# Row minima of two strips by ScalarE copies and GpSimd halvings, every block transpose on VectorE, row buffers as scratch for the late spans: one change to a four-layer network kernel

## The chip, the cores and the metric

The kernel runs on one core of one Trainium2 chip. The metric is the device time of one execution in microseconds; the figure for the kernel before is the median of three runs. A core has TensorE (PE: matrix products, results into PSUM), VectorE (DVE), ScalarE (ACT), GpSimd (POOL, which here works only on SBUF tiles) and SyncE (SP, which issues the transfers). Each engine takes its own instructions strictly in the order written and waits on semaphores for the others.

## The reference

A sequence of 2048 tokens of 128 numbers passes through four layers. Each layer adds an attention of a layer-normalised x to x, and then adds a feed-forward of a layer-normalised x.

- L0: full softmax attention, 16 heads of 64; then a mixture of 8 experts with a capacity limit.
- L1: causal attention, 16 heads of 64; then a gated mix of each token with the token before it (`r * (relu(k)^2 @ W_v)`).
- L2: an "attention" whose query and key terms are such that the kernel needs only one 128x128 product per token (the folded matrix `w2`); then a feed-forward of width 512 with ternary weights and ReLU.
- L3: full attention with a region mask and a bias per head and query from five small feature networks; then a feed-forward of width 512 with binarised weights and an exact GELU.

For full attention with queries q, keys k and values v of one head:

```
scores[i, j] = q_i . k_j / 8        (+ mask, + bias)
p[i, :]      = exp(scores[i, :] - max_j scores[i, j])
out[i]       = sum_j p[i, j] v_j / sum_j p[i, j]
```

Everything is float32 except small mask tiles.

## The kernel before

**Attention.** Heads go two at a time: 8 pairs in each of the layers L0, L1 and L3. In a pair, class `Pair` makes kT, qT and v from the normalised, transposed x (`projected`, L450 and `valued`, L471). The queries of a pair are cut into 8 groups of 256, and a group into 8 strips of 32 queries. Class `Group` holds the work of one group. So a full layer has 64 groups, the two full layers (L0 and L3) 128.

The kernel keeps scores negated (qT is multiplied by -scale), so that the row maximum of the softmax is a row minimum here. The keys are spread out: partition block c (of four, 32 partitions each) holds the 32 queries of the strip against every fourth block of 32 keys, 512 of the 2048 keys. For one strip and one head the scores are thus a PSUM bank of 128 partitions by 512.

The steps of a group, with the lines that the profile names:

1. `score` / `make` (L556, PE): two strips times two heads fill four PSUM banks. The ring `BANKS` has just four.
2. `scan` (L566, DVE): one instruction per strip and head copies the bank into the row buffer `e` in SBUF and takes the minimum of each row at the same time, into `low`. 16 scans in a group.
3. `spread_lowest`: POOL sets the four partition blocks' minima side by side (L613), DVE reduces them (L616), in L3 POOL subtracts and adds the bias (L620, L621), and ACT (in L1 POOL) hands the result out to the partition blocks (L627). Once for strips 0 to 3 (j = 0) and once for strips 4 to 7 (j = 1).
4. `exps` (L639, ACT): exponentials in place, with row sums, 16 in a group.
5. `turn` (L666, DVE): the exponentials are transposed in 32x32 blocks in place. There is one call per half (j) and head (h), 128x2048 each. In the full layers the last of the four calls (j = h = 1, `apart`) does only 384 of the 512 columns of each strip, 128x1536; the other 128 columns go through four PE transposes (L674) and an ACT copy back from PSUM (L677). A PE transpose gives another order of the keys in the partitions, so those columns need a copy `va` of the values with rows in that order: `regroup` (L485, POOL), 16 small copies per pair.
6. `weigh` (L698, PE): values times turned exponentials, accumulated in the bank `o`, in four steps of eight matmuls.
7. `sum_up` (L719 and POOL's power L739), the copy oT (L771, ACT), the output projection (L756, PE), the division (L766, ACT) and the addition to x (L784, POOL).

**Between L1 and L3** the tokens go in spans of 4, 4, 4, 2 and 2 tiles of 128. Each span runs `first_norm`, then `rest`: the gated mix of L1, the product of L2, the ternary feed-forward, and three more calls of `normalise`; at the end stands the x that L3's keys and queries are made of. L3's softmax needs all keys, so its first score waits for the last span. Scratch tiles come from rings with few buffers: `MIXED` 3 (one span takes all three), `PAIRED` 2, `MID` 4, and the PSUM ring `MISC` 3. `features` makes L3's bias from the same x, in four chunks. At the end of the program `final` runs L3's feed-forward over the same spans.

`normalise` takes statistics on DVE (L301 to L303), then three POOL instructions (add epsilon L306, power -1/2 L307, multiply by minus the mean L308), then scales on ACT (L311) and on DVE or POOL (L316), transposes on PE (L322) and copies to xT on ACT (L337).

**The order of the work** is not written out by hand. Every step is an object with an engine, an assumed duration, what it needs and which ring buffers it takes. A planner (`run`) plays a list schedule forward and ranks the steps backward from their latest starts, three times over, and the best of these gives the order in which each engine's instructions are written. `planner(tick, place)` gives the first rank. So a change of a step's engine or assumed cost can move instructions everywhere.

Of the kernel before, what the change touches and what calls it, by code (L numbers as in the profile page):

```python
# [13 lines left out]
ALU = mybir.AluOpType  # L14
AX = mybir.AxisListType

P = 128
# [41 lines left out]
def network(ctx: ExitStack, tc: tile.TileContext, a: dict, out: bass.AP):  # L59
# [26 lines left out]
    class Held:  # L86


        def __init__(self, ring, called=None):
            self.ring, self.called, self.users = ring, called, []  # L90

    class Step:
        def __init__(self, key, engine, us, do, after=(), takes=(), uses=(), then=None, table=None):
            self.key, self.engine, self.us, self.do, self.takes = key + (len(steps),), engine, us, do, takes
            self.table = table
            self.after, self.order, self.then, self.end = list(after), [], then, None
            for h in takes:
                h.by = self
                h.users.append(self)
                h.ring.takers.append(self)  # L100
            for h in uses:
                self.after.append(h.by)
                h.users.append(self)
            steps.append(self)
# [15 lines left out]
    def run():  # L120
# [101 lines left out]
        for _ in range(3):  # L222
            rank = backward()
            if not forward(rank, False):
                break
            found.append((max(s.end for s in steps), len(found), rank))
# [13 lines left out]

    MISC = Ring(ps_t, "t", [P, 512], 3, ordered=False)
# [8 lines left out]
    APART = Ring(work, "va", [P, 4, DH], 2)  # L250
# [43 lines left out]
    def normalise(add, t0, n, after, before=(), row=None, hurry=False):  # L294


        mv, xn, pt = Held(MEANS), Held(NORMED), Held(MISC, "pt")

        def stats(i):
            st = small.tile([P, 6], F32, tag="st", name="st")  # L300
            nc.vector.bn_stats(out=st, in_=x[:, t0 + i, :])  # L301
            nc.vector.bn_aggr(out=mv.t[:, i, 0:2], in_=st)
            nc.vector.tensor_scalar(mv.t[:, i, 3:4], mv.t[:, i, 0:1], -1.0, None, ALU.mult)  # L303
# [20 lines left out]
        made = [add(DVE, 0.6, lambda: stats(0), after, takes=[mv])]  # L324
        made += [add(DVE, 0.6, lambda i=i: stats(i), after, uses=[mv]) for i in range(1, n)]
        power = add(POOL, 1.65, powers, made, uses=[mv])
        scales = [add(ACT, 0.45, lambda: scaled(0), [power], takes=[xn], uses=[mv])]
        for i in range(1, n):
            if i < n // 2:
                scales.append(add(ACT, 0.4, lambda i=i: scaled(i), [power], uses=[mv, xn]))  # L330
            elif hurry:
                scales.append(add(DVE, 0.3, lambda i=i: scaled_on(nc.vector, i), [power], uses=[mv, xn]))
            else:
                scales.append(add(POOL, 0.8, lambda i=i: scaled_on(nc.gpsimd, i), [power], uses=[mv, xn]))
# [20 lines left out]
    class Attention:  # L355
# [31 lines left out]
        def course(self, p):  # L387
# [15 lines left out]
            if p == HP - 1:  # L403
                groups = [(g, 4 * g, 4 * g + {0: 12, 1: 10}.get(g, 8)) for g in range(NS)]
                return groups, 0, (-5, 3, 11, 19), steady, (9, 13, 18, 24)
# [11 lines left out]
        def left(self, t0, n):  # L417

            groups = self.course(HP - 1)[0]
            g, _, weigh = groups[(t0 + n - 1) // 2]  # L420
            return self.begin + 32 * (HP - 1) + weigh + (g // 2 + 1 if self.causal else 4) + 1
# [4 lines left out]
    class Pair:  # L426
# [39 lines left out]
        def valued(self, add, c):  # L466
# [13 lines left out]
            if c == 3 and not self.layer.causal:  # L480
                self.va = Held(APART)

                def regroup(i):
                    for q in range(4):
                        nc.gpsimd.tensor_copy(self.va.t[bass.ts(i, Q), q, :], v.t[bass.ts(q, Q), i, DH:P])  # L485

                self.va_made = [
                    add(
                        POOL, 1.0, lambda i=i: regroup(i), self.v_made[3:],
                        takes=[] if i else [self.va], uses=[v, self.va] if i else [v],  # L490
                    )
                    for i in range(4)
                ]

    class Group:
# [37 lines left out]
        def score(self, add, add_scan, k):  # L533
# [47 lines left out]
            for i in range(2):  # L581
                for h in range(2):
# [5 lines left out]
                    (uses if k % 2 or i or h else takes).append(self.lows[j])  # L588
                    found.append(
# [4 lines left out]
            return found  # L594

# [57 lines left out]
        def apart(self, j, h):  # L653

            return j == h == 1 and not self.layer.causal

        def turn(self, add, j, h, made):


            n = self.width(4 * j) - (P if self.apart(j, h) else 0)  # L660

            def rows():
                return self.e(h)[:, bass.ts(j, 4), :]

            def do():
                nc.vector.transpose(rows()[:, :, 0:n], rows()[:, :, 0:n])  # L666

            turned = [add(DVE, 0.05 + 0.00426 * n, do, made, uses=self.rows)]
            if self.apart(j, h):
                pt = Held(MISC)  # L670

                def turn_apart():
                    for i in range(4):
                        nc.tensor.transpose(pt.t[:, bass.ts(i, P)], rows()[:, i, n : n + P], ident)  # L674

                def copy():
                    nc.scalar.copy(rows()[:, :, n : n + P], pt.t.rearrange("p (i n) -> p i n", i=4))  # L677

                add(PE, 0.55, turn_apart, made, takes=[pt], uses=self.rows)
                turned.append(add(ACT, 0.47, copy, uses=[pt] + self.rows))  # L680
            return turned

        def weigh(self, add, c, turned):
# [7 lines left out]
            def do():  # L691
                for t in ts:
                    for h in range(2):
                        parts = [(first(t), NS, self.pair.v[c].t[:, t % 4, bass.ds(DH * h, DH)])]
                        if c == 3 and self.apart(1, h):
                            parts = [(0, 4, parts[0][2]), (4, NS, self.pair.va.t[:, t % 4, :])]
# [11 lines left out]
            if c == 3 and self.apart(1, 1):  # L708
                uses, made = uses + [self.pair.va], made + self.pair.va_made
# [323 lines left out]
    def feed_forward(add, t0, n, after, full, w1T, b1, func, w2T):  # L1033

        hT, made, po = [Held(MID, "hT") for f in range(NC)], [], Held(MISC, "po")
        for f in range(0, NC, 2):
            ph = [Held(MISC, "ph") for k in range(2)]
# [121 lines left out]
    def rest(add, t0, n, done, hurry, made):  # L1159
        m = P * n  # L1160
        xr, xk, ka, r = Held(MIXED, "xr"), Held(MIXED, "xk"), Held(MIXED, "ka"), Held(PAIRED, "r")
        pk, pr, pv, po = (Held(MISC, n) for n in ("pk", "pr", "pv", "po"))
# [24 lines left out]
        for to, part, mu in ((xk, rests[1], mu_k), (xr, rests[0], mu_r)):  # L1187
# [44 lines left out]
        done, rows = normalise(add, t0, n, [full], read, row=ob2, hurry=hurry)  # L1232
# [5 lines left out]
        done, rows = normalise(add, t0, n, [full] + rows, [attended], row=b2_2, hurry=hurry)  # L1238
# [3 lines left out]
            lambda: ternary_w.t[:, 0:FF], b1_2, AF.Relu, lambda: ternary_w.t[:, FF : 2 * FF],  # L1242
# [3 lines left out]
        done, rows = normalise(add, t0, n, [full] + rows, firsts, row=ob3, hurry=hurry)  # L1246
# [132 lines left out]
    mix_spans = [(0, 4), (4, 4), (8, 4), (12, 2), (14, 2)]  # L1379
# [7 lines left out]
    for t0, n in mix_spans:  # L1387
# [3 lines left out]
    for t0, n in mix_spans:  # L1391
        rest(planner(L1.left(t0, n)), t0, n, done[t0], n < 4, made)
    feature_reads = []
    for c in range(4):
        seen = len(steps)
        features(planner((L1.left(8, 4) - 1, L1.left(12, 2) - 1, L1.left(14, 2) + 1, L1.left(14, 2) + 2)[c]), c)
# [95 lines left out]
```

## Time and profile before

| what | value |
|---|---|
| time, median of 3 runs | 3460.41 us (3458.63 to 3462.35) |
| the profiled execution: time, and span from first to last instruction | 3458.86 us, 3457.2 us |
| busy: PE, DVE, ACT, POOL | 3371.3, 3216.3, 2801.9, 950.9 us |
| L0, four pairs from 392.94 to 983.91 us | 147.74 us per pair |
| L3, two pairs from 2350.89 to 2649.92 us | 149.5 us per pair |
| end of L1's last `weigh` to L3's first score | 2120.09 to 2204.46 us |

The span is the time between the first and the last instruction of one profiled execution; the rest of that execution's time lies around it. A record of a matmul has a modelled end, and one float32 product shows as two records, so counts of PE instructions in the profile are twice those of the program. Durations of neighbouring instructions overlap a little in the records; the distance from start to start is what an instruction really takes from its engine. A group's idle time is the idle time of its engine just before it, with what ended it.

### The profile page before, as it was taken

The page shows a single profiled execution, that of the slowest core. Times are in us where ns is not written, and L with a number is a line of the kernel's source. Part 1 is how long each engine was busy: PE and PEld are TensorE (multiplying, and loading weights), DVE is VectorE, ACT ScalarE, POOL GpSimd, SP SyncE. Part 2 cuts the span into 40 slices and gives each one's busy share as a digit, 9 for nine tenths or more (in the row PEclk, how much of TensorE's full clock was granted, in tenths as well). Part 3 has the DMA queues.
Part 4 walks back from the last instruction along what each step waited for, and adds up shares of the span by engine and source line. Part 5 has one row for each costly group of instructions (what it writes and reads, how often), then busy time and mean ns, then how long its engine had stood idle before and what let it go on. Part 6 is the DMA issues. An engine that isn't in the chain of part 4 may idle for free.

```text
span 3457.2 us, 115453 instructions
## 1 busy us (share of the span) xinstructions
PE 3371.3 (98%) x46922; PEld 1808.7 (52%) x46922; DVE 3216.3 (93%) x8019; ACT 2801.9 (81%) x8707; POOL 950.9 (28%) x2821
## 2 busy tenths in 40 slices
PE   8999999999999998999999997899999999999999
PEld 3544444545445454555655654455555555555555
DVE  7999999999999989899999884699999999999996
ACT  6788888888888777788888985678888888888886
POOL 2121221222222343233233353222222222222233
PEclk9999999999999999999999998899999999999999
DMA  1000000000000000000000000000000000000000
GB/s 48 2 5 2 5 5 2 5 2 5 2 5 5 2 5 8 6 6 6 6 6 3 9 2 4 4 5 5 2 5 2 5 5 2 5 2 2 2 5 11
DMA packets 22961, 18.98 MB, mean 5 GB/s; under 512 B 3557, under 2 KB 21613, under 8 KB 22427
## 3 DMA queue, kind: packets, MB, share of 16 engines
q1 hardware_dynamic: 22362, 11.55, 1.2%
q8 instruction: 367, 6.01, 0.7%
q14 instruction: 168, 1.37, 0.1%
q0 software_dynamic: 64, 0.06, 0.0%
HBM read 10.60 MB, written 1.05 MB: 3 GB/s over the span
## 4 chain that ended last, share of the span: by engine, by line
PE 83%; DVE 12%; ACT 3%; issue 2%; POOL 0%; DMA 0%; SPq 0%; DVEq 0%; POOLq 0%; ACTq 0%
PE s L556 33%; PE o L698 32%; DVE e L566 6%; PE pp L450 5%; DVE e L666 4%; PE y L756 3%; PE pv L471 3%; PE t L674 2%; ACT e L639 1%; PE ps L719 1%; PE pe L999 1%; PE ph L1041 1%; PE po L1066 1%; PE pt L322 0%; DVE st L301 0%
## 5 line engine op out<-in xcount | busy, mean ns | idle before, releaser
L639 ACT ACTIVATE e<-e,shift 128x512 f32<-128x512 f32 (+15 forms) x3072 | 1972.7, 648 | 23.7 <-POOL shift L627 16.4
L566 DVE TENSOR_SCALAR_CACHE_REDUCE e<-s 128x512 f32<-128x512 f32 (+15 forms) x3072 | 1660.5, 590 | 77.9 <-PE s L556 75.1
L556 PE MATMUL s<-kT,qT 64*32 64x512 f32 (+8 forms) x24576 | 1448.9, 533 | 17.7 <-DVE e L566 16.4
L666 DVE STREAM_TRANSPOSE e<-e 128x2048 f32<-128x2048 f32 (+10 forms) x768 | 1436.8, 1873 | 18.8 <-ACT e L639 18.0
L698 PE MATMUL o<-e,v 128*64 128x256 f32 (+1 forms) x10496 | 1275.4, 374 | 6.6 <-DVE e L666 6.4
L698 PEld LDWEIGHTS o<-e,v 128*64 128x64 f32 x10496 | 738.4, 137 | 565.5 <-issue 309.3
L556 PEld LDWEIGHTS s<-kT,qT 64*32 64x32 f32 x24576 | 413.7, 105 | 527.0 <-DVE e L566 218.0
L639 ACT ACTIVATION_READ_ACCUMULATOR e<-e,shift 128x1 f32 x3072 | 592.3, 193 | 0.0
L613 POOL COPY low<-low 32x8 f32<-32x8 f32 x1152 | 208.1, 181 | 1336.3 <-DVE e L566 1238.9
L784 POOL TENSOR_TENSOR x<-x,part 128x256 f32<-128x256 f32 x384 | 280.5, 730 | 359.2 <-ACT part L766 338.2
L627 ACT COPY shift<-shift 32x8 f32<-32x8 f32 x768 | 150.0, 195 | 178.9 <-POOL shift L621 98.5
L766 ACT ACTIVATE part<-y,r 128x128 f32<-128x128 f32 x768 | 220.6, 360 | 42.7 <-PE y L756 38.4
L566 DVE DVE_READ_ACCUMULATOR e<-s 128x1 f32 x3072 | 235.0, 76 | 0.0
L450 PE MATMUL pp<-xT,w 128*128 128x512 f32 x384 | 212.7, 646 | 2.5 <-ACT xT L337 1.9
L698 PE MATMUL o<-e,va 128*64 128x128 f32 x1024 | 196.4, 274 | 0.0
L739 POOL TENSOR_TENSOR r<-r,inverse 128x4 f32<-128x4 f32 x128 | 130.2, 1017 | 171.6 <-ACT r L742 169.7
L771 ACT COPY oT<-o 128x256 f32<-128x256 f32 x192 | 71.0, 370 | 125.1 <-PE o L698 124.6
L556 PE MATMUL s<-beyond,eye 64*32 64x32 bf16 x2560 | 158.2, 176 | 0.0
L756 PE MATMUL y<-w,oT 64*128 64x128 f32 x1536 | 137.9, 297 | 1.0 <-ACT oT L771 0.7
L756 PEld LDWEIGHTS y<-w,oT 64*128 64x128 f32 x1536 | 100.9, 186 | 57.5 <-issue 46.5
L698 PEld LDWEIGHTS o<-e,va 128*64 128x64 f32 x1024 | 126.8, 138 | 0.0
L556 PEld LDWEIGHTS <-regions 64*32 64x32 bf16 x1024 | 65.3, 93 | 112.2 <-issue 78.5
(190 smaller groups left out, 2055.0 us busy)
## 6 DMA issues: line engine op xcount, KB each, us to landing
w<-in_L_wq SPq DMA_DIRECT2D x24, 64.0 KB
w<-in_L_wk SPq DMA_DIRECT2D x24, 64.0 KB, 2.1
w<-in_L_wv SPq DMA_DIRECT2D x24, 64.0 KB
w<-in_L_wo SPq DMA_DIRECT2D x24, 64.0 KB, 2.1
x<-in_x SPq DMA_DIRECT2D x4, 256.0 KB, 4.8
out_x<-x SPq DMA_DIRECT2D x3, 256.0 KB
wo<-in_L_wo SPq DMA_DIRECT2D x1, 512.0 KB
moe_w<-in_moe_w SPq DMA_DIRECT2D x1, 512.0 KB
```

The source lines that it names most:

```text
L450: nc.tensor.matmul(pp.t, lhsT=self.w.t[:, which, :], rhs=xT[:, cols(4 * c, 4)], start=True, stop=True)
L556: nc.tensor.matmul(s[h].t[on, bass.ds(first, size)], lhsT=lhsT, rhs=rhs, start=m == 0, stop=m == len(terms) - 1,)
L566: nc.vector.tensor_scalar(self.e(h)[:, i, 0:n], s.t[:, 0:n], 1.0, None, ALU.mult, ALU.min, accum_out=self.lows[j].t[:, 0, 4 * h + i % 4 : ...
L613: nc.gpsimd.tensor_copy(low.t[0:Q, c], low.t[bass.ts(c, Q), 0])
L627: (nc.gpsimd.tensor_copy if causal else nc.scalar.copy)(shift.t[bass.ts(c, Q)], first())
L639: nc.scalar.activation(e, e, AF.Exp, bias=self.shifts[j].t[:, 4 * h + i % 4 : 4 * h + i % 4 + 1], scale=-1.0, accum_out=self.sums.t[:, h, ...
L666: nc.vector.transpose(rows()[:, :, 0:n], rows()[:, :, 0:n])
L698: nc.tensor.matmul(self.o.t[bass.ds(DH * h, DH), i0:i1, :], lhsT=lhsT, rhs=self.e(h)[:, i0:i1, bass.ts(t, Q)], start=t == 0, stop=t == las ...
L739: nc.gpsimd.tensor_tensor(some, some, inverse, ALU.pow)
L756: nc.tensor.matmul(y[h].t[:, bass.ts(j, P)], lhsT=oT.t[half, bass.ts(j, P)], rhs=pair.w.t[half, 3, :], start=True, stop=True,)
L766: nc.scalar.mul(part.t[:, j, :], y[h].t[:, bass.ts(j, P)], r.t[:, j, h : h + 1])
L784: POOL, 0.8, lambda part=part: nc.gpsimd.tensor_tensor(xs, xs, part.t, ALU.add), [divided], uses=[part]
```

## The change

1. **Two of the sixteen scans of a group in the full layers** (strip 1 and strip 5, second head: `BY_COPY`) are no longer VectorE instructions. ACT copies the bank to the row buffer. POOL takes the minimum by halvings: of columns 0 to 255 and 256 to 511, then of the two halves of the result; each halving is a subtraction, a minimum with zero and an addition. VectorE then reduces the remaining 128 columns to the minimum.
2. **All block transposes of the full layers are on VectorE**: `apart`, the PE transposes, their ACT copy, `va` and its ring and `regroup` are gone.
3. **Late spans** (those from tile 8 on) take the scratch of `rest` out of one row buffer (`room`, cut by the new class `Part`) in place of `MIXED`, `PAIRED` and `MID`, and their PSUM banks from `BANKS` in place of `MISC`; such tiles are `loose`, which leaves them out of the fixed order of takers of the ring. Their rank is set to the end of L1.
4. **A shorter layernorm** for the hurried spans of two tiles: VectorE adds epsilon, POOL does only the power, and VectorE does both scalings.
5. The last pair of L1 has other due times (`course`), `left` computes when a span's groups are done over all groups of the span, `features` chunks 0 and 1 have earlier ranks, and the planner makes five passes in place of three.

```diff
+    class Part:
+        def __init__(self, whole, first, n):
+            self.whole, self.on = whole, bass.ds(first, n)
...
-        for _ in range(3):
+        for _ in range(5):
...
+    BY_COPY = ((1, 1), (5, 1))
...
-    APART = Ring(work, "va", [P, 4, DH], 2)
+    LESSER = Ring(small, "lesser", [P, 256], 2)
...
+        short = hurry and n < 4
...
-            nc.vector.tensor_scalar(mv.t[:, i, 3:4], mv.t[:, i, 0:1], -1.0, None, ALU.mult)
+            if not short:
+                nc.vector.tensor_scalar(mv.t[:, i, 3:4], mv.t[:, i, 0:1], -1.0, None, ALU.mult)
+            elif i == n - 1:
+                nc.vector.tensor_scalar(mv.t[:, 0:n, 2], mv.t[:, 0:n, 1], EPS, None, ALU.add)
+
+        def power_alone():
+            nc.gpsimd.tensor_tensor(mv.t[:, 0:n, 2], mv.t[:, 0:n, 2], half_power[:, 0:n], ALU.pow)
...
-                groups = [(g, 4 * g, 4 * g + {0: 12, 1: 10}.get(g, 8)) for g in range(NS)]
-                return groups, 0, (-5, 3, 11, 19), steady, (9, 13, 18, 24)
+                groups = [(g, 4 * g, 4 * g + 12 - g // 2) for g in range(NS)]
+                return groups, 0, (-5, 7, 15, 23), steady, (9, 10, 11, 12)
...
-            if c == 3 and not self.layer.causal:
-                self.va = Held(APART)
...
+                    if not causal and (2 * k + i, h) in BY_COPY:
+                        found.append(self.compare(add_scan, 2 * k + i, h, banks[i][h], takes, uses))
+                        continue
...
+        def compare(self, add, i, h, s, takes, uses):
+            low = Held(LESSER)
+
+            def lesser(n):
+                a = self.e(h)[:, i, :] if n == 256 else low.t
+                b, a = a[:, 0:n], a[:, n : 2 * n]
+                less = low.t[:, 0:n]
+                nc.gpsimd.tensor_tensor(less, b, a, ALU.subtract)
+                nc.gpsimd.tensor_scalar(less, less, 0.0, None, ALU.min)
+                nc.gpsimd.tensor_tensor(less, less, a, ALU.add)
+
+            copied = add(ACT, 0.5, lambda: nc.scalar.copy(self.e(h)[:, i, :], s.t), takes=takes, uses=uses)
+            rows = self.rows[h : h + 1]
+            add(POOL, 2.2, lambda: lesser(256), [copied], takes=[low], uses=rows)
+            last = add(POOL, 1.6, lambda: lesser(128), uses=[low])
+
+            def lowest():
+                found = self.lows[i // 4].t[:, 0, 4 * h + i % 4 : 4 * h + i % 4 + 1]
+                nc.vector.tensor_reduce(found, low.t[:, 0:128], AX.X, ALU.min)
+
+            return add(DVE, 0.2, lowest, [last], uses=[low, self.lows[i // 4]])
...
-            n = self.width(4 * j) - (P if self.apart(j, h) else 0)
...
+            n = self.width(4 * j)
...
-                add(PE, 0.55, turn_apart, made, takes=[pt], uses=self.rows)
-                turned.append(add(ACT, 0.47, copy, uses=[pt] + self.rows))
...
-                        if c == 3 and self.apart(1, h):
-                            parts = [(0, 4, parts[0][2]), (4, NS, self.pair.va.t[:, t % 4, :])]
...
+        if apart:
+            room = Held(ROWS, "room")
+            xr, xk, ka, r = (Part(room, m * k, m) for k in range(4))
+        bank = BANKS if apart else MISC
+        pk, pr, pv, po = (Held(bank, n, apart) for n in ("pk", "pr", "pv", "po"))
...
-        rest(planner(L1.left(t0, n)), t0, n, done[t0], n < 4, made)
+        late = t0 >= 8
+        rest(planner(*((L1.begin + 255, 50 + t0) if late else (L1.left(t0, n),))), t0, n, done[t0], n < 4, made, late)
```

## The prediction

> **What bounds the kernel now.** First the page: the busy shares of the whole span, then the forty slices.
>
> ```profile
> PE 3371.3 (98%) x46922; PEld 1808.7 (52%) x46922; DVE 3216.3 (93%) x8019; ACT 2801.9 (81%) x8707; POOL 950.9 (28%) x2821
> ...
> PE   8999999999999998999999997899999999999999
> ...
> DVE  7999999999999989899999884699999999999996
> ```
>
> Two engines are full nearly everywhere, POOL is nearly empty, and there is a dip in slice 24 to 25 (about 2100 to 2200 us), between L1 and L3. A PE record can be stretched by waiting, so I went to busy time by stretch: four pairs of L0, two of L3, the tail of L1, and what DVE waits for in those L0 pairs.
>
> ```profile
> 392.94:983.91 590.97, 590.97 (x7496) 290.91 (x7499) 586.51 (x1217) 501.35 (x1488) 128.53 (x352) 1.00 0.01 4
> ...
> 2350.89:2649.92 299.03, 299.03 (x4024) 158.56 (x4028) 295.33 (x618) 247.76 (x744) 76.75 (x240) 1.00 0.01 4
> ...
> 2120.00:2204.50 84.50, 61.09 (x244) 36.98 (x241) 29.18 (x115) 35.71 (x75) 29.24 (x51) 0.78 0.03 7
> ...
> DVE e L566 <- PE s L556: 4.0, 4, 1.0
> ```
>
> Columns: stretch, length, busy PE, PE weight load, DVE, ACT, POOL, granted clock. L0 has 147.74 us per pair, and DVE works 146.6 of them; it rests once a pair, for 1 us. DVE bounds L0. In L3 the period is 149.5 and DVE works 147.7. PE's timeline there has a score step every 2.05 us (mask matmuls ride along; 1.88 in L0). Per pair PE needs 32 x 2.05 score steps, 32 x 1.88 weighs, 8 kT and qT products at 1.05, 4 v at 1.09, 8 x 0.53 transposes, 8 x 0.24 and 8 x 0.65: 65.6 + 60.2 + 8.4 + 4.4 + 4.2 + 1.9 + 5.2 = 149.9. So PE bounds L3, with DVE close. The same sum for L0 is 144.5, 3 us under its period. In the tail neither bounds: PE rests 23.4 of 84.5 us at a clock of 0.78.
>
> **Part 1 and 2, VectorE.** From DVE's timeline in L0, start to start:
>
> ```profile
> 840.74 0.67 DVE L566 TENSOR_SCALAR_CACHE_REDUCE e<-s 128x512 f32<-128x512 f32 x1
> 841.35 0.07 DVE L566 DVE_READ_ACCUMULATOR e<-s 128x1 f32 x1
> 841.35 0.19 DVE L616 TENSOR_REDUCE shift<-low 32x8 f32<-32x32 f32 x1
> 841.47 2.29 DVE L666 STREAM_TRANSPOSE e<-e 128x2048 f32<-128x2048 f32 x1
> 843.70 0.64 DVE L566 TENSOR_SCALAR_CACHE_REDUCE e<-s 128x512 f32<-128x512 f32 x1
> ```
>
> A scan takes 0.61, a whole transpose 2.23, the 128x1536 one 1.69 (837.24 to 838.93). A 128x128 reduce is a row (L1335, 260 ns); the small reduce above shows 0.19 and costs 0.12, so I take 0.19 for the new one (0.12 to 0.26). Per group: -2 x 0.61 + 0.54 + 2 x 0.19 = -0.30; per pair -2.4. L0 goes to 146.6 - 2.4 + 1 (the rest that stays) = 145.2, a gain of 2.5.
>
> **TensorE.** The four transposes go, 0.53 a group, 4.2 a pair; the split weigh with `va` took 1.90 against 1.88, another 0.2. In L3 PE then needs 149.5 - 4.4 = 145.1 and DVE 147.7 - 2.4 = 145.3. With both at the same height I add 0.9 of mutual waiting, near the 1.1 that L0 shows: 146.2, a gain of 3.3. Eight pairs each: 20 + 26 = 46 us. Between 2 x 8 x 2.4 = 38 (DVE alone) and 2 x 8 x 3.3 = 53 lies the range of this term.
>
> **ScalarE.** Out goes one copy (L677, 0.48 start to start), in come two of the same form: +0.48 a group, +3.9 a pair. ACT's 125.3 a pair becomes 129 of 145, 89%. Hidden by its own idle time, but each copy stands in ACT's queue behind exponentials (0.70 each), and the PE's next strip waits for the bank.
>
> **GpSimd, the new wait.** The rows nearest to the halvings:
>
> ```profile
> L784 POOL TENSOR_TENSOR x<-x,part 128x256 f32<-128x256 f32 x384 | 280.5, 730 | 359.2 <-ACT part L766 338.2 <-DVE shift L616 7.2
> ...
> L316 POOL TENSOR_SCALAR xn<-x,mv 128x128 f32<-128x128 f32 x46 | 36.5, 801 | 0.7
> ...
> L306 POOL TENSOR_SCALAR mv<-mv 128x4 f32<-128x4 f32 x27 | 6.4, 239 | 81.7 <-DVE mv L302 81.7
> L1021 POOL TENSOR_TENSOR parts<-parts 128x128 f32<-128x128 f32 x16 | 7.3, 456 | 1.3
> ```
>
> With 0.08 between dependent POOL instructions the four two-input ones are 2 x 0.81 + 2 x 0.53 = 2.7. The minimum with a constant at 256 and 128 columns is not in the trace. Below: 0.24 each, the price at 4 columns; above: the slope of L316, which has two operations and operands from memory, 4.5 ns a column: 1.4 and 0.8. I take 0.6 and 0.4, under the two-input rows of the same width, since one input less has to be read. A chain is then 3.8 us (3.3 to 5.0). POOL gains 16 x 3.8 - 3.7 (`regroup`, 16 x 0.23) = 57 a pair on 32: 61% of 145 (up to 75%). It doesn't become the bound.
>
> What counts is whether a chain is back before VectorE reaches its reduce, since all DVE work queues behind that. In the order of the changed program's instructions the strip is scored after the scan that frees its last bank; from there DVE has, for strip 1, a transpose, three scans, the small reduce, a transpose and three scans: 2.23 + 1.8 + 0.12 + 2.23 + 1.8 = 8.2 us. For strip 5 it is one scan less, 7.6. The chain needs 1.0 (half a score step and its semaphore) + 0.7 (ACT copy) + 3.8 + 0.1 = 5.6, with the upper price 6.9. So 2.6 and 2.0 us are left, 1.3 and 0.7 at the upper price: I cost the wait at nothing. An ACT copy that is late by two exponentials (1.4) is covered at 3.8, not at 5.0. In L3 the bias instructions of the group before (L620, L621) stand behind a chain in POOL's queue, and the exponentials' shift waits for them: some 2 us later, but DVE transposes these exponentials 3.6 us later than that by the same order.
>
> **A rule that speaks against this.** First the rows: from 867.41 to 868.95 POOL runs two L784 additions; the scans at 867.22, 867.83 and 868.44 take 0.68, 0.67 and 0.67, and the transpose at 841.47 under another addition 2.29, its usual length. And POOL works 32 of 147.74 us a pair. The Trainium skill, "GPSIMD Engine Reference", section "4.1 Engine selection", says to keep elementwise work on VectorE, since GpSimd takes about twice as long for two inputs; and "SBUF — State Buffer", section "Who interferes with whom", that the two share a port pair under an exclusive lock, which some DVE forms wait for. By the first, taken as it stands, the edit pays 7.6 us for 1.2: 128 x 6.4 = +820 us if POOL's time lay on the path. By the second, if scans and transposes were such forms, 128 x 7.6 = +970. The rows say that POOL's time lies beside DVE's and doesn't lengthen it: nothing. I take the rows; of the rules stays that the chain is long, which rival 3 prices.
>
> **Part 3 and 5, the late spans.** PE's timeline in the tail shows where it rests.
>
> ```profile
> 2132.91 1.54 PE L322 MATMUL pt<-ident,xn 128*128 128x128 f32 x6 [6.67 <-ACT xn L311]
> 2135.13 2.08 PE L1183 MATMUL po<-w,xT 128*128 128x128 f32 x8 [0.67 <-ACT xT L337]
> 2142.68 1.50 PE L322 MATMUL pt<-ident,xn 128*128 128x128 f32 x4 [5.47 <-ACT xn L311]
> 2144.91 6.06 PE L1041 MATMUL ph<-xT,ternary_w 128*128 128x512 f32 x8 [0.73 <-ACT xT L337]
> ```
>
> One span walks alone through layernorms (PE waits 6.67 and 5.47 us), and the matmuls after each wait run at half clock (the same two `ph` steps took 1.95 and 1.91 at 2084.79 and 2088.62; here 6.06). One set of `MIXED` scratch keeps the next span back. The changed order interleaves the steps of the three last spans there, and moves the product and feed-forward of the span at tile 4 behind L1's last weigh. Counting its PE instructions by these rows, the tail holds about 60 us of work, some 14 of it moved in from a stretch where PE was 95% busy (2040 to 2120), which that stretch loses. If all waits went, 64 us: gain 84 + 13 - 64 = 33. If 23 us of waits and 6 of slow clock stayed, 89: gain 8. I take the middle, 20. The row buffers are free then, as L1's groups end.
>
> **Part 4, the short layernorm.** POOL's three instructions (0.23 + 0.72 + 0.20, two tiles wide) become one, 0.72; about 0.6 us each in the chain of the last spans, inside the 20 above; one stands at the end of the program: -1.
>
> **Ramps.** At the start of L0 and L3 nothing hides the first chains, and after L3's last scans neither: about 4 us of latency, of which the next group's scans cover half, two or three times: +4.
>
> **Sum against the profiled execution.** 3458.9 - 46 - 20 - 1 + 4 = 3396 us (its span 3457.2, 1.7 around it). The median of runs is 1.5 above it: 3397. The terms of the tail and of mutual waiting lean on the hopeful side, so I write 3400.
>
> **Rivals.**
>
> 1. *Only part arrives.* PE and DVE at the same height hold each other up, or late ACT copies hold banks, so that pairs gain half of 46, and the new order of L1's end gains only 8 and loses some at another joint: 3460 - 23 - 8 + 0 to 4 = 3430 to 3450. For it: L3 with both at 99% already shows more loss (1.8 us) than L0.
> 2. *No change the clock can tell.* The ring of four banks sets the pace whatever the engines need: 3460. Against: DVE rests only 4.5 in 591 us.
> 3. *Slower: reduces wait for POOL.* Place: the new reduce at the head of DVE's queue, with transposes and scans behind it, which PE (banks) and the weighs wait for. At a chain of 5.0 and ACT copies late by 1.4, strip 5's need is 8.3 against 7.6 and strip 1's 8.3 against 8.2: 0.8 a group, 128 x 0.8 = 102 us, 3400 + 102 = 3502. It decides once a reduce waits 60 / 256 = 0.23 us in the mean. For it: a price that the trace lacks, and ACT at 89%. Against: the slack above.
>
> **How the numbers follow.** Chances: the main case 0.6 (own range 3380 to 3425), rival 1 0.2, rival 2 0.06, rival 3 0.14. The predicted time is the main case's, 3400 us. The range runs from 3365 (all terms at their good ends: 53 + 33) to 3465, with rivals 1 and 2 inside; what is left out is mostly rival 3. 0.2% of 3460 is 7 us, about what a measurement of this kernel tells from no change: faster 0.8, same 0.06, slower 0.14.
>
> **What would show it.** Right: L0 periods of 145 and L3 of 146 us; DVE still over 99% busy there with waits for PE only, none on POOL at the new reduce; chains of 3.8 us; POOL near 55% over the whole; a tail of 64 to 80 us without PE waits over 5 us. Wrong: idle DVE before the 128x128 reduce with POOL as releaser, L566 or L666 longer than 0.67 and 2.29, halvings with a minimum over 1 us, or ACT copies that PE's scores wait for.

## The result, and the profile after

| | before | after |
|---|---|---|
| median | 3459.52 us | 3424.83 us (3424.31 to 3428.94) |
| ratio | | 0.9902, 95% interval 0.9885 to 0.9919 |
| span of the profiled execution | 3457.2 us | 3427.2 us |
| start to L1's first masked score (L0) | 1243.7 | 1231.0 (-12.7) |
| L1, first to last masked score | 837.9 | 829.2 (-8.7) |
| from there to L3's first masked score | 123.7 | 108.3 (-15.4) |
| L3, first to last masked score | 1203.5 | 1212.7 (+9.2) |
| from there to the end | 48.4 | 46.0 (-2.4) |
| a steady pair of L0, of L3 | 147.7, 149.5 | 146.9, 150.2 |

The kernel is 1% faster: 35 us, where I had forecast 60. L1 and the stretch behind it gave 24 us, a little more than I had put on the late spans. L0's pairs gave a third of their forecast, and L3's became longer.

First the page after, busy shares and slices:

```profile
PE 3361.0 (98%) x45386; PEld 1687.4 (49%) x45386; DVE 3189.6 (93%) x7763; ACT 2846.3 (83%) x8826; POOL 1838.0 (54%) x4081
...
PE   7999999999999999999999998999999999999998
...
DVE  7999999999999989899999996799999999999996
```

The dip of PE in slices 24 and 25 is now one slice of 8. POOL has doubled, to 54%, near the 55% that I had expected. Next, busy time by stretch: four pairs of L0, then two of L3 (columns as before: PE, PE weight load, DVE, ACT, POOL, clock).

```profile
326.99:914.55 587.56, 587.56 (x7112) 257.55 (x7119) 578.54 (x1153) 512.03 (x1520) 352.12 (x673) 1.00 0.01 4
...
2311.30:2610.93 299.63, 299.63 (x3833) 146.72 (x3825) 290.46 (x578) 254.58 (x765) 187.26 (x400) 1.00 0.01 4
```

DVE works 144.6 us of each L0 pair, and I had forecast 144.2. So its work fell as it should; but it now rests 2.3 us a pair where it rested 1.1. In L3 it works 145.2 of 149.8 (the fastest of these two pairs took 149.4) and rests 4.6, where it rested 1.9. What it waits for in these four L0 pairs, in these two L3 pairs, and over the whole program (us in total, times, longest):

```profile
DVE low L643 <- POOL lesser L634: 7.1, 20, 0.8
DVE e L590 <- PE s L580: 1.9, 4, 0.5
...
DVE low L643 <- POOL lesser L634: 5.8, 14, 0.9
DVE e L590 <- PE s L580: 2.5, 6, 0.6
...
DVE e L590 <- PE s L580: 63.7, 112, 6.5
DVE low L643 <- POOL lesser L634: 42.1, 96, 1.2
```

The row with L643 is new: the new reduce waits for GpSimd's halvings, 7.1 / 4 = 1.8 us in an L0 pair, 5.8 / 2 = 2.9 in an L3 pair, and over the program in 96 of 256 cases. That is the row that I had named as the sign of being wrong. The mean over all 256 is 42.1 / 256 = 0.16 us. The halvings by shape (busy, mean ns, idle before):

```profile
L633 POOL TENSOR_SCALAR lesser<-lesser 128x256 f32<-128x256 f32 x256 | 217.1, 848 | 22.4
...
L632 POOL TENSOR_TENSOR lesser<-e 128x256 f32<-128x256 f32 x256 | 187.5, 732 | 418.4 <-ACT e L636 392.2 <-ACT r L768 24.9
...
L633 POOL TENSOR_SCALAR lesser<-lesser 128x128 f32<-128x128 f32 x256 | 134.1, 524 | 22.4
...
L643 DVE TENSOR_REDUCE low<-lesser 128x1 f32<-128x128 f32 x256 | 70.6, 276 | 44.2 <-POOL lesser L634 42.1
```

The minimum with a constant takes 0.85 and 0.52 us, where I had taken 0.6 and 0.4. From first start to last end a chain takes 4.17 us in the mean of the 66 chains of L0 that start between 330 and 930 us, against my 3.8. Now one such wait in the timeline of L0, all engines in order of time, cut to one strip (between the exponentials stand the readings of their row sums, left out here):

```profile
850.09 1.95 PE L580 MATMUL s<-kT,qT 64*32 64x512 f32 x32
...
851.41 0.71 ACT L690 ACTIVATE e<-e,shift 128x512 f32<-128x512 f32 x1
...
852.11 0.71 ACT L690 ACTIVATE e<-e,shift 128x512 f32<-128x512 f32 x1
...
852.82 0.71 ACT L690 ACTIVATE e<-e,shift 128x512 f32<-128x512 f32 x1
...
853.52 0.71 ACT L690 ACTIVATE e<-e,shift 128x512 f32<-128x512 f32 x1
...
854.23 0.57 ACT L636 COPY e<-s 128x512 f32<-128x512 f32 x1
...
854.94 0.74 POOL L632 TENSOR_TENSOR lesser<-e 128x256 f32<-128x256 f32 x1 [3.65 <-ACT r L768]
...
858.65 0.46 POOL L634 TENSOR_TENSOR lesser<-lesser 128x128 f32<-128x128 f32 x1
...
859.14 0.29 DVE L643 TENSOR_REDUCE low<-lesser 128x1 f32<-128x128 f32 x1 [0.42 <-POOL lesser L634]
```

DVE was through with the scan that frees the last bank at 850.46. From there it had a transpose, three scans, the small reduce, a transpose and three scans to do, and was through at 858.72: 8.26 us, as I had counted (8.2). The other side of the account is off:

| from 850.46 | predicted | here |
|---|---|---|
| until the scores are done | 1.0 | 1.58 (852.04) |
| the copy stands behind exponentials | 0 (1.4 as the upper case) | 2.19: the rest of one, then three |
| copy to chain | 0.7 | 0.71 |
| chain | 3.8 | 4.17 |
| to the reduce | 0.1 | 0.03 |
| sum | 5.6 | 8.68 |

8.68 against 8.26 is the 0.42 us in the last line.

This is one strip, and its copy is later than most. The same account as a mean of those 66 chains, counted from the end of the scores (strip 5's chain on the right):

| after the scores are done | strip 1: predicted, mean | strip 5: predicted, mean |
|---|---|---|
| the copy begins | 0, 1.88 | 0, 0.86 |
| copy to chain | 0.7, 0.69 | 0.7, 0.73 |
| chain | 3.8, 4.17 | 3.8, 4.17 |
| the chain is back | 4.5, 6.75 | 4.5, 5.76 |
| VectorE is at the reduce | 7.2, 6.89 | 6.6, 5.83 |

So hardly any slack was left in the mean, and single chains fall on either side of it: 21 of the 66 reduces waited.

Last, two of PE's rows in the tail, which answer to the four shown of before: its longest wait for the layernorms of the late spans, and eight `ph` steps.

```profile
2101.24 0.66 PE L350 MATMUL pt<-ident,xn 128*128 128x128 f32 x2 [2.74 <-DVE xn L344]
...
2138.93 3.60 PE L1070 MATMUL ph<-xT,ternary_w 128*128 128x512 f32 x8
```

The waits of 6.67 and 5.47 us are gone, and eight records take 3.60 us, at a granted clock of 1.00, where they took 6.06 at 0.61.

### The profile page after: what moved, and what is told of

It is laid out like the page before. It is cut to its first block, busy times and chain, and to the rows that moved or that the text cites. A ratio compares the mean times of both kernels' runs of the same rounds, so it can differ in the third digit from the quotient of the medians.

```text
span 3427.2 us, 113447 instructions
## 1 busy us (share of the span) xinstructions
PE 3361.0 (98%) x45386; PEld 1687.4 (49%) x45386; DVE 3189.6 (93%) x7763; ACT 2846.3 (83%) x8826; POOL 1838.0 (54%) x4081
## 4 chain that ended last, share of the span: by engine, by line
PE 77%; DVE 9%; ACT 7%; POOL 5%; issue 2%; DMA 0%; SPq 0%; POOLq 0%; DVEq 0%; ACTq 0%
PE s L580 32%; PE o L726 30%; PE pp L488 5%; ACT e L690 4%; DVE e L590 4%; PE y L782 3%; DVE e L709 3%; PE pv L509 3%; POOL lesser L633 1%; POOL lesser L634 1%; POOL lesser L632 1%; PE ps L745 1%; PE po L1095 1%; PE pe L1025 1%; PE ph L1070 1%
## 5 line engine op out<-in xcount | busy, mean ns | idle before, releaser
L590 DVE TENSOR_SCALAR_CACHE_REDUCE e<-s 128x512 f32<-128x512 f32 (+14 forms) x2816 | 1517.8, 583 | 65.5 <-PE s L580 63.7
L709 DVE STREAM_TRANSPOSE e<-e 128x2048 f32<-128x2048 f32 (+10 forms) x768 | 1505.9, 1963 | 21.5 <-ACT e L690 20.7
L580 PE MATMUL s<-kT,qT 64*32 64x512 f32 (+8 forms) x24576 | 1479.9, 533 | 16.8 <-DVE e L590 13.7
L726 PE MATMUL o<-e,v 128*64 128x256 f32 (+1 forms) x10496 | 1312.6, 385 | 7.7 <-DVE e L709 7.4
L632 POOL TENSOR_TENSOR lesser<-e 128x256 f32<-128x256 f32 x256 | 187.5, 732 | 418.4 <-ACT e L636 392.2
L633 POOL TENSOR_SCALAR lesser<-lesser 128x256 f32<-128x256 f32 (+1 forms) x512 | 351.2, 686 | 44.9
L590 DVE DVE_READ_ACCUMULATOR e<-s 128x1 f32 x2816 | 219.3, 78 | 0.0
L634 POOL TENSOR_TENSOR lesser<-lesser,e 128x256 f32<-128x256 f32 x256 | 187.6, 733 | 21.4
L636 ACT COPY e<-s 128x512 f32<-128x512 f32 x256 | 146.8, 573 | 21.9 <-PE s L580 21.9
L678 POOL COPY shift<-shift 32x8 f32<-32x8 f32 x384 | 70.2, 183 | 167.3 <-DVE shift L667 140.6
L765 POOL TENSOR_TENSOR r<-r,inverse 128x4 f32<-128x4 f32 x128 | 132.3, 1034 | 24.1 <-ACT r L768 21.8
```

The costliest lines, as they stand in the source:

```text
L580: nc.tensor.matmul(s[h].t[on, bass.ds(first, size)], lhsT=lhsT, rhs=rhs, start=m == 0, stop=m == len(terms) - 1,)
L590: nc.vector.tensor_scalar(self.e(h)[:, i, 0:n], s.t[:, 0:n], 1.0, None, ALU.mult, ALU.min, accum_out=self.lows[j].t[:, 0, 4 * h + i % 4 : ...
L632: nc.gpsimd.tensor_tensor(less, b, a, ALU.subtract)
L633: nc.gpsimd.tensor_scalar(less, less, 0.0, None, ALU.min)
L634: nc.gpsimd.tensor_tensor(less, less, a, ALU.add)
L678: (nc.gpsimd.tensor_copy if causal else nc.scalar.copy)(shift.t[bass.ts(c, Q)], first())
```

## The experiments

The first theory: the time of a chain, from the copy to the reduce, ate the gain of the pairs. The rivals: the work of the engines was counted wrongly, or the bias step behind the chain in L3 is to blame.

**A short chain.** Of each halving only the subtraction is left; the minimum and the addition are left out, so what reaches the reduce isn't the row minimum. The order of all other work is the changed kernel's, since the planned prices stay.

```
-                nc.gpsimd.tensor_scalar(less, less, 0.0, None, ALU.min)
-                nc.gpsimd.tensor_tensor(less, less, a, ALU.add)
```

> Left out: of each halving on POOL only the subtraction is done, so the minima handed on are not the rows' minima and the output is not the reference's; the order of everything else is that of the changed kernel. A chain on POOL falls from 4.3 us (0.73 + 0.85 + 0.73 + 0.46 + 0.52 + 0.46 with gaps) to about 1.4. Theory A (the length of the chain took the expected gain: reduces wait on DVE, and in L3 the shift waits behind the chain): L0 pairs go from 146.9 to 145.2 us, L3 pairs from 150.2 to 146.2, the whole from 3425 to about 3380. Rival B (PE and DVE at the same height hold each other up through the four banks, whatever POOL does): both periods stay within 0.5 us, the whole at 3425. Rival C (ScalarE, 89% busy with the copies, bounds L3): L0 gains up to 1.7, L3 stays at 150.

Measured, one execution: 3385.79 us, L0 pairs of 145.0, L3 pairs of 146.9. The stretches of four L0 pairs and two of L3 in that run:

```profile
322.61:902.41 579.80, 579.80 (x7112) 255.24 (x7118) 576.73 (x1153) 511.49 (x1520) 188.64 (x417) 1.00 0.01 4
2288.60:2582.32 293.72, 293.72 (x3832) 143.00 (x3824) 289.21 (x578) 254.60 (x763) 105.47 (x272) 1.00 0.01 4
```

DVE rests 0.8 us in an L0 pair, and no wait for POOL's halvings is left. So the engines' work was counted rightly (145.2 and 146.2 forecast), and the time of the halvings took the rest: 39 us against the changed kernel. ScalarE as the bound of L3 falls too, since L3's pairs became shorter with all its copies in place. From first to last masked score of L3 this run takes 1187.7 us, the change 1212.7, and my forecast came to 1203.5 - 26 = 1177.5. So 25 of the 35 us between forecast and result are the halvings' time; the other 10 are not, and some 7 of them lie in one pair (L3's fifth, below).

**No bias step.** L3's two small GpSimd instructions behind the chain are left out (the shift then lacks the rounding that they give it); the step stays in the planning, so the order is the same.

```
-                nc.gpsimd.tensor_tensor(to, to, b, ALU.subtract)
-                nc.gpsimd.tensor_tensor(to, to, b, ALU.add)
+                pass
```

> Left out: the two POOL instructions that put L3's bias into the shift, so L3's shift is without the bias term; everything else and its order as in the changed kernel. In L3 the shift then goes from DVE's reduce straight to ScalarE and no longer stands behind a chain in POOL's queue. Theory A1 (in L3 the loss is the bias standing behind the chain, so that ScalarE's exponentials start late): L3 pairs from 150.2 to about 147, L0 pairs unchanged at 146.9, the whole near 3400. Theory A2 (in L3 too it is the DVE reduce that waits for the chain): L3 stays above 149. Rival B: L3 stays at 150.

Measured, one execution: 3413.21 us, L3 pairs 148.8 (from 150.2), L0 unchanged. The bias step is a part, 1.4 us a pair, and not the whole: without the long chain L3 stands at 146.9.

**The price in the planning.** The changed kernel plans a chain at 2.2 + 1.6 = 3.8 us. The planner puts the reduce where it believes the chain to be back. Only these two numbers are changed, first to what the instructions take:

```
-            add(POOL, 2.2, lambda: lesser(256), [copied], takes=[low], uses=rows)
-            last = add(POOL, 1.6, lambda: lesser(128), uses=[low])
+            add(POOL, 2.55, lambda: lesser(256), [copied], takes=[low], uses=rows)
+            last = add(POOL, 1.7, lambda: lesser(128), uses=[low])
```

> Only the planner's assumed durations of the two halvings change, 2.2 to 2.55 and 1.6 to 1.7 us, which is what they measure with their gaps; the work is the same. Theory A with the misjudged price as its cause: the planner puts each reduce later and the waits of DVE on POOL, 42 us in all, fall under 15; the whole 10 to 25 us faster than the changed kernel, 3400 to 3415. If the loss is latency that no order hides: within 8 us of 3425. Rival B: no change.

A single better order could be luck. So the prices went to 1.85 and 1.5, to 2.9 and 2.0, and to 3.5 and 2.5:

> Only the two prices of a halving in the order's planning change, 2.2 and 1.6 to 1.85 and 1.5: a chain is planned at 3.35 us where it takes about 4.3 (the changed kernel plans 3.8). Theory P (the misjudged price makes VectorE wait for GpSimd): more such waits than the changed kernel's 42 us, L3 pairs of 150.5 us or more, 3430 to 3445 us. Theory N (any new price gives another order, and 4.25 happened on a better one): time scatters between 3405 and 3440 and doesn't go with the waits.

> Only the two prices change, to 2.9 and 2.0: a chain is planned at 4.9 us where it takes about 4.3. Theory P: VectorE's waits for GpSimd fall below the 16.9 us of true prices, and the time stays within 6 us of 3409, since what is left above the run with short chains is PE and VectorE holding each other up. Theory N: anything from 3405 to 3440.

> The two prices go to 3.5 and 2.5: a chain is planned at 6.0 us where it takes about 4.3. Theory P (waits of VectorE for GpSimd are what a price that is too low costs): those waits are about gone (under 10 us), so nothing is left to win; the time stays at 3400 to 3410, or rises by 5 to 15 us because a row of scores is now held longer than need be. If still more came back (under 3393), the waits were not the whole of the price's effect.

| chain planned at | time | ratio to before | DVE's waits for the halvings | L0, L3 pair |
|---|---|---|---|---|
| 3.35 us | 3489.94 | 1.009 (1.0073 to 1.0107) | 113.0 us | 150.5, 154.3 |
| 3.8 (the change) | 3424.83 | 0.9902 (0.9885 to 0.9919) | 42.1 | 146.9, 150.2 |
| 4.25 | 3408.94 | 0.9859 (0.9842 to 0.9875) | 16.9 | 145.9, 147.1 |
| 4.9 | 3401.22 | 0.9837 (0.9822 to 0.9851) | 10.4 | 146.1 to 149.3, 146.2 to 147.9 |
| 6.0 | 3459.97 | 1.0005 (0.9996 to 1.0015) | 0.3 | 149.6, 151.3 to 152.3 |

At the low price, the waits in four pairs of L0 (325 to 925 us) are in one row:

```profile
DVE low L643 <- POOL lesser L634: 24.0, 28, 1.3
```

24.0 / 4 = 6.0 us a pair, and 144.5 of work + 6.0 is the period of 150.5. The same kernel with the same instructions is then slower than before. At the price of 4.9 the two rows of waits, over the whole program, are

```profile
DVE e L590 <- PE s L580: 78.8, 122, 10.6
...
DVE low L643 <- POOL lesser L634: 10.4, 23, 0.9
```

and at 6.0 the second is down to 0.3 us, once, and the first has grown, in the whole program and in four L0 pairs:

```profile
DVE e L590 <- PE s L580: 123.9, 196, 9.8
DVE e L709 <- ACT e L690: 46.7, 51, 4.0
...
DVE e L590 <- PE s L580: 19.9, 36, 1.3
```

There the reduce comes 2.3 us (L0) and 3.0 us (L3) after the end of its chain in the mean, and DVE waits for scores instead: 19.9 / 4 = 5.0 a pair, 144.6 + 5.0 = 149.6. So up to 4.9 the time of the whole program goes with the waits. Layer by layer (us):

| chain planned at | waits for the halvings in L0, L3 | start to L1's first masked score | L3, first to last masked score |
|---|---|---|---|
| 3.35 | 41.0, 72.0 | 1258.3 | 1240.0 |
| 3.8 | 14.4, 27.7 | 1231.0 | 1212.7 |
| 4.25 | 5.8, 11.1 | 1231.4 | 1192.4 |
| 4.9 | 8.9, 1.5 | 1235.4 | 1187.6 |

L3 follows its waits. Ahead of L1 neither higher price gains on the change, though L0's steady pairs are 1 us shorter at 4.25. And from 4.25 to 4.9 the stretch behind L3's last masked score alone becomes 10.5 us shorter, more than the whole gain of 8.

At 4.25 the waits fell to 16.9, where I had expected under 15, and the time came out as expected (3400 to 3415); at 4.9 it is 2 us below the range that I gave. The low price cost far more than the 3430 to 3445 us that I had expected of it. Above 4.9 a second loss takes over, larger than the 5 to 15 us that I had allowed; theory P was too mild there. Which buffer makes PE's scores late in that order I didn't isolate. That ScalarE's copies wait 88 us for scores, against 22, and the transposes 46.7 for exponentials, against 20.7, fits a row whose minimum is fetched late.

**The parts alone.** L3 with its scans, PE transposes and `va` as before, L0 as changed:

```
+    AS_BEFORE = ("L3",)
...
-                    if not causal and (2 * k + i, h) in BY_COPY:
+                    if not causal and layer.name not in AS_BEFORE and (2 * k + i, h) in BY_COPY:
...
+            return j == h == 1 and self.layer.name in AS_BEFORE
```

> L0 as in the changed kernel; L3's attention as before (sixteen scans on DVE, the last transpose partly on PE, va in the buffers of lesser). L3 took 1203.5 us before (first to last mask matmul) and takes 1212.7 in the changed kernel. Theory A and rival C (parts 1 and 2 cost L3 time): L3 pairs back at 149.5, the first one 146, the whole 3412 to 3420. If the longer L3 comes from what the late spans hand over and not from parts 1 and 2: 3425 or more.

(`va` is back as well; it takes its buffers from the ring `LESSER`.) And both full layers as before, so that only parts 3 to 5 are changed: late spans, short layernorm, due times and passes of the planner (the edit is the same with `("L0", "L3")`, and `va` has its own ring again):

> Parts 3 to 5 alone: attention of both full layers as before (sixteen scans on DVE, the last transpose partly by PE with va), the late spans, the short layernorm, the due times and the five passes as in the changed kernel. From the two profiles the stretch from L1's first masked score to L3's first gained 24 us and the end 2.4. If parts 3 to 5 stand alone: L0 pairs 147.7, L3 pairs 149.5, the whole 26 us (20 to 32) under before, near 3432, so that parts 1 and 2 together were worth only about 7. If that gain needed parts 1 and 2 (PE freed of transposes, DVE of scans at the end of L0): under 15 us, above 3443.

Measured: 3415.03 us (3410.86 to 3420.33; ratio 0.9878, 0.9864 to 0.9893) and 3427.48 us (0.9909, 0.9894 to 0.9924). With L3 as before its pairs are back at 149.5 and the kernel is 8 to 10 us faster than the change (by the ratios, by the medians): in L3 the copies and halvings, in this order, cost time. Parts 3 to 5 alone give 31 to 32 of the change's 35 us; which of them gives how much, no run separates. L1 takes 827.8 and the stretch to L3 107.6, as in the change. Parts 1 and 2, on which I put 46 us, are worth about 3 together, no more than the intervals of the two ratios leave open: L0's gain is spent in L3.

**L3's fifth pair.** In the change it takes 158.4 us, 8.2 more than its neighbours; before 152.2, 2.7 more. VectorE makes binary weights there. My theory was that this work stands on the path, as the reduces behind it wait. The work is left out, and with it the weights' signs:

```
-                    nc.vector.tensor_reduce(alpha, part, AX.X, ALU.add, apply_absolute_value=True)
...
-                    nc.vector.tensor_tensor(part, part, sign, ALU.add)
+                    pass
```

> Left out: VectorE's 30 instructions that binarise the last layer's weights (L1369 to L1377), so the last feed-forward uses the raw weights; order and all else as in the changed kernel. They stand in one run of 9.7 us in L3's fifth pair, which takes 158.4 us where its neighbours take 150.2; before, that pair took 152.2 and its neighbours 149.5. If DVE is now the engine without slack (Theory A with DVE as the bound): that pair falls to 150 to 151 and the whole by about 8, to 3417. If the pair is long for another cause (its weights' transfers, the PE transposes of the weights): it stays over 156.

Measured, one execution: 3427.27 us, the pair at 159.4: the theory fell. Where the work had been, DVE now only waits:

```profile
2764.53 2.29 DVE L709 STREAM_TRANSPOSE e<-e 128x2048 f32<-128x2048 f32 x1
2772.37 0.69 DVE L590 TENSOR_SCALAR_CACHE_REDUCE e<-s 128x512 f32<-128x512 f32 x1 [5.55 <-PE s L580]
...
2776.26 0.29 DVE L643 TENSOR_REDUCE low<-lesser 128x1 f32<-128x128 f32 x1 [1.97 <-POOL lesser L634]
```

The scores stand where the plan put them in PE's queue, behind other PE work, with or without DVE's; and behind them the next reduce again waits for its chain. With the chain planned at 4.9 us, all the work in place, this pair takes 149.4, 3.2 more than 146.2. At 4.25 it still takes 155.5; and with the short chain, where no reduce waits, 156.8, 9.9 more than its neighbours. So most of the 8.2 belongs to the order, then, neither to the work nor to the chain. This pair alone makes 6.2 of the 9.2 us by which L3 became longer.

**One halving.** GpSimd halves once, VectorE reduces 256 columns (planned at 0.33 us in place of 0.2):

```
-            add(POOL, 2.2, lambda: lesser(256), [copied], takes=[low], uses=rows)
-            last = add(POOL, 1.6, lambda: lesser(128), uses=[low])
+            last = add(POOL, 2.55, lambda: lesser(256), [copied], takes=[low], uses=rows)
...
-                nc.vector.tensor_reduce(found, low.t[:, 0:128], AX.X, ALU.min)
+                nc.vector.tensor_reduce(found, low.t, AX.X, ALU.min)
```

> One halving on GpSimd instead of two, VectorE then reduces 256 columns (about 0.13 us more each, 16 a pair: 2.1 us), planned at 2.55 and 0.33. A chain takes 2.5 us instead of 4.3. Theory C (length of chain took the gain, VectorE's work was the limit in L0): L0 pairs of 144.7 + 2.1 + 0.3 = 147 us, no better than the changed kernel, L3 pairs of 147.5 to 148.5, 3405 to 3415 us. If latency alone counted and VectorE's work didn't: L0 145, L3 147, near 3390 us.

Measured: 3426.54 us (0.9907, 0.9893 to 0.9922), pairs of 147.9 and 148.7. The reduce takes 394 ns where it took 276: 16 x 0.12 = 1.9 us a pair, and DVE works 586.4 / 4 = 146.6 of 147.9. L0 is then no better than before, as expected within 1 us; the total is 11 above the range that I gave. Latency alone isn't the bound in L0: DVE's work is, once the chain is short.

**Prices with the bias step left out,** from the instructions and from the planning, at 4.25 and at 4.9:

```
-            if self.layer.bias is not None:
-                made = add(POOL, 0.42, with_bias, [made] + self.layer.biased[self.g // 2], uses=[shift])
```

> The planner's true prices of the halvings, as in the run with them alone, and L3's two bias instructions left out together with their step (subtracting and adding the same bias changes the shift only by rounding, and the softmax doesn't depend on the shift). Theory A: L3 pairs go from 147.1 to 145.5 to 146.5, L0 pairs as in the run with the true prices, 145.9; the whole 3396 to 3404. If the true prices have already taken everything the bias cost: within 4 us of 3409.

> Prices of 2.9 and 2.0, and L3's two bias instructions on GpSimd left out (they round the shift; every shift of L3 then lacks that rounding). If the bias step still delays L3's exponentials at these prices: L3 pairs of 145 to 145.7 and 3393 to 3398 us. If the higher price has already hidden it: 146.2 as with the price alone, 3398 to 3403 us.

Measured: 3402.56 us (0.9838, 0.9822 to 0.9855), L3 pairs of 148.1; and 3411.36 us (0.9863, 0.9847 to 0.988), L3 pairs of 148.0. The first total lies in the range that I gave (3396 to 3404), but not by way of L3's pairs, for which I had expected 145.5 to 146.5; the second misses in both. With less to do L3's pairs are longer by 1.0 and 1.8 us than at the same price with the step. Taking a step out of the planning makes another order, and that order is the poorer one in L3. So among good orders some 10 us are the planner's luck, and the 8 us between 4.25 and 4.9 can't be put down to the price alone. The run with the step kept in the planning (3413 against 3425, one execution) is the only clean one on the bias.

The fastest full version is the change with its chain planned at 4.9 us: 3401.22 us, 23.6 below the change, 56 below before.

## Why the prediction was right and where it was wrong

Right within its range (3365 to 3465), 25 us too hopeful at its point. The mechanism held where VectorE's work fell and where the late spans moved, not in the two layers on which 46 of the 60 us were put: about 3 of these came. That the total still fell in the range is in part luck: the same edit with its chain planned at 3.35 us takes 3490, outside it.

- *VectorE's work* (-2.4 a pair): right. 144.6 us of work in an L0 pair; with a short chain its period is 145.0 where 145.2 was forecast.
- *TensorE and mutual waiting in L3* (146.2): right as a limit, 146.9 with the short chain and 146.2 to 147.9 at a planned 4.9. It wasn't reached in the change.
- *GpSimd, "I cost the wait at nothing"*: the step that failed. Three terms of the account were off in the mean of 66 chains of L0: the copy behind exponentials (0 in the main case, 1.4 as the upper one; 1.88 for strip 1 and 0.86 for strip 5), the chain (3.8; 4.17, from a minimum priced below its neighbours), and VectorE's own way to the reduce (0.3 and 0.8 shorter than counted). Together they use up the slack of 2.6 and 2.0 us. In L0 this left 0.8 us of the forecast 2.5 a pair; in L3 it turned a gain of 3.3 into a loss of 0.7, and the fifth pair comes on top. Over the layers: 12.7 gained in place of 20 ahead of L1, 9.2 lost in place of 26 gained in L3.
- *What I hadn't asked*: where the order gets its slack from. I read the place of the reduce from the written order as if it were a fact of the kernel. It follows from the planned price of 3.8 us, which was itself too low. The rows of prices show it: the slack is set by one number, too little or too much.
- *Scans and transposes beside GpSimd*: right. They take 0.67 and 2.29 us as before, with POOL working 60% of an L0 pair. Only if the rule of the port pair held for them would it have made +970 us of this; the Trainium skill, "SBUF — State Buffer", section "Who interferes with whom", says that a VectorE instruction with at most one SBUF input, outside the modes that use two ports, does not contend with GpSimd, and scans (from PSUM) and transposes read no second SBUF tile.
- *The late spans* (20): 24.1 measured over L1 and the stretch behind it. *The end* (1): 2.4. *Ramps* (4): no run isolates them.
- *Rival 1* (only part arrives, 3430 to 3450) ends 5 us above the result. It was too hopeful of the pairs (half of 46, where 12.7 - 9.2 = 3.5 came) and too shy of the late spans (8, where 24.1 came).
- *Rival 3* (slower, decided once a reduce waits 0.23 us in the mean) was the mechanism at work, below its point: 0.16. Its sum was off by 0.1: 1.0 + 0.7 + 5.0 + 0.1 is 6.8, not 6.9, which makes 77 us of its 102. The run at the low price is beyond it, 113.0 / 256 = 0.44 us, and is slower than before by 0.9%.

## What to carry to other kernels

When work is moved from a full engine to an idle one, count the whole way to the result and back: the queue ahead of the first step, the new instructions, and what the full engine has queued behind the wait. An idle engine with a dear instruction adds no work to the path but adds latency, and the slack for it lies in the order. If a planner makes that order, measure the new step and put its true price in before judging the change; then try prices on both sides, as some microseconds of any single result are the order's luck.

## What the runs showed of the hardware

A minimum with a constant on GpSimd is dearer than an operation with two tensors of the same size: 848 against 732 ns at 128x256, 524 against 456 at 128x128. I had assumed the opposite.

Some VectorE forms do slow down beside GpSimd, only not those that fill L0. In L3's fifth pair of the changed kernel, VectorE's timeline and GpSimd's:

```profile
2765.51 0.71 DVE L1377 TENSOR_TENSOR w<-w,low 128x128 f32<-128x128 f32 x1
...
2767.49 0.70 DVE L1377 TENSOR_TENSOR w<-w,low 128x128 f32<-128x128 f32 x1
...
2769.46 0.29 DVE L1377 TENSOR_TENSOR w<-w,low 128x128 f32<-128x128 f32 x1
...
2765.19 0.88 POOL L810 TENSOR_TENSOR x<-x,part 128x256 f32<-128x256 f32 x1
2767.17 0.87 POOL L810 TENSOR_TENSOR x<-x,part 128x256 f32<-128x256 f32 x1 [1.10 <-ACT part L792]
```

The addition with two SBUF operands takes 0.71 and 0.70 us where it lies under a GpSimd addition, and 0.29 where it lies alone; the GpSimd additions take 0.88 and 0.87 against a mean of 0.73. The scalar-tensor-tensor instruction just before each (L1376) also reads two SBUF tiles and lies mostly under the same addition, but it starts 0.06 and 0.07 us before it, and keeps its 0.35. The Trainium skill, "SBUF — State Buffer", section "Who interferes with whom", states that a VectorE instruction with two SBUF inputs contends with a GpSimd instruction that reads SBUF, and that the order of issue decides who waits. Both agree with these two cases; no run here varies the order.
